# Decay sums of a selective-state scan: one f32 product against three products of exact bfloat16 parts

## The chip, the cores and the metric

The kernel runs on one core of one Trainium2 chip. The metric is the device time of one execution in microseconds. A core has a matrix engine (TensorE, PE in the profile, with its weight loads shown apart as PEld), a vector engine (DVE), a scalar engine (ACT), a general engine (POOL), and SP, which issues the DMA transfers. Each engine runs its instructions in order, and they meet through semaphores. SBUF is the on-chip memory of 128 partitions, PSUM the accumulators that TensorE writes.

## The reference

One layer of a model on 16 sequences of 32 tokens with 512 channels, all in float32, in three stages: a graph attention over a context, a Mamba-2 scan, and a feed-forward part with low-rank additions. The change lies in the scan, cut here to what it concerns:

```python
dt = jax.nn.softplus(dt + dt_bias)                 # per token and head, 128 heads
A = -jnp.exp(A_log)
Ac = (A * dt) ...                                  # one number per token and head
L = jnp.exp(segsum(Ac))                            # L[i, j] = exp(sum of Ac over j < t <= i), 0 for j > i
M = jnp.einsum('bcihn,bcjhn->bcijh', Ch, Bh) * L   # 8 groups of 16 heads share B and C
Y_diag = jnp.einsum('bcijh,bcjhp->bcihp', M, hid * dt)
y = Y_diag + D * hid
y = y * silu(gate), normalized within each group, then the output projection
```

A sequence has 32 tokens, shorter than one chunk, so the part that passes states between chunks contributes nothing.

## The kernel before

The 512 tokens lie as four blocks q of 128 tokens (four sequences each). The 8192 inner channels are 64 tiles t of 128 channels, two heads each; a group g has TG = 8 such tiles. The code is written with a tile framework: the program allocates tiles from pools and calls engine operations, and at compile time a scheduler orders every engine's instructions by the order of the program and by when, in its own model, operands and buffers are ready. It also inserts the semaphores. An engine's order on the chip is then fixed.

Before the groups, `scan_part` loads constants and makes the two masks on POOL: `le`, 1 where token j comes no later than token i in the same sequence, and `gt`, 1 where a token comes later. `lei` is `le` folded to 128 x 32: for each token of a block, which of the 32 positions of its sequence are at or after it. It projects `dt` and makes `dA` = dt times A for all tokens and heads (L1170), and makes `CB` for each group, the product of B and C with the mask (L1186).

Then, for each group, in program order:

- `inner(g + 1)`: for each of the 8 tiles, `project` (L1120) makes the gate and the hidden channels of the next group, each with four f32 matmuls of 128x128 by 128x512, and `convolve` runs the short causal convolution on ACT and DVE (L1127, L1132, L1135). Their PSUM pool has two buffers; the tiles `gs` and `hid` have two buffers of a whole group.
- `mix(g)`: for each tile, four transposes (`pht`, L1228), `hd` on DVE (L1230, dt times the transposed channels), the decays (every second tile, for its four heads), two `el` on DVE (L1241, the decays times `CB`), eight small matmuls `py` (L1249), then `hid` (L1253) and `gs` (L1254) on DVE, their squares on ACT (L1259), and their sum `ssq` on POOL (L1260).
- `close(g)`: `pn` (L1268) sums `ssq` across partitions, DVE and ACT make the inverse norm `gr`, and `po` (L1281) is the output projection, 4 token blocks of 8 f32 matmuls, each accumulated into `xt` by DVE (L1284). Its PSUM pool has two buffers.

`decays(h)` serves four heads, that is a pair of tiles; it runs 32 times. POOL multiplies `lei` and the `dA` of four heads, both broadcast, into `da`, 128 x 512 in f32 with two buffers (L1208). PE multiplies that by the mask `gt` (L1213), which sums dA over the tokens after j up to i. ACT takes the exponential into `ed` (L1218). An f32 `nc.tensor.matmul` appears in the profile as two matmul instructions and two weight loads.

The PSUM pool `ps_m` that `pl` comes from has two buffers, shared with the transposes.

Of the kernel before, what the change touches and what calls it, by code (L numbers as in the profile page):

```python
# [8 lines left out]
F32 = mybir.dt.float32  # L9
F16 = mybir.dt.float16  # L10
BF16 = mybir.dt.bfloat16
I32 = mybir.dt.int32
AF = mybir.ActivationFunctionType
ALU = mybir.AluOpType
# [4 lines left out]
P = 128  # L19
# [21 lines left out]
H_M, G_M, SEQ = 128, 8, 32  # L41
# [11 lines left out]
def kernel(ctx: ExitStack, tc: tile.TileContext, I, out):  # L53
# [68 lines left out]
    with ExitStack() as cx:  # L122
        scan_part(nc, tc, cx, I, id32, ones, xt, U, rstd, lows)
# [931 lines left out]
def scan_part(nc, tc, cx, I, id32, ones, xt, u, rstd, lows):  # L1055


    sc = cx.enter_context(tc.tile_pool(name="sconst", bufs=1))
    wk = cx.enter_context(tc.tile_pool(name="swk", bufs=2))
    sm = cx.enter_context(tc.tile_pool(name="ssm", bufs=3))  # L1060
# [27 lines left out]
    gt = sc.tile([P, P], F32, name="gt")  # L1088
# [10 lines left out]
    lei = sc.tile([P, SEQ], F32, name="lei")  # L1099
# [47 lines left out]
    dA = sc.tile([P, 4, H_M], F32, name="dA")  # L1147
# [44 lines left out]
    def inner(g):  # L1192
# [9 lines left out]
                next(parts, None)  # L1202
        return gs, hid

    def decays(h):

        da = sm.tile([P, 4, 4, SEQ], F32, tag="da", name=f"da{h}", bufs=2)
        nc.gpsimd.tensor_tensor(  # L1208
            da, lei.unsqueeze(1).unsqueeze(1).to_broadcast([P, 4, 4, SEQ]),
            dA[:, :, h:h + 4].rearrange("p q h -> p h q").unsqueeze(3).to_broadcast([P, 4, 4, SEQ]), ALU.mult,  # L1210
        )
        pl = ps_m.tile([P, 4, 4, SEQ], F32, tag="m", name=f"pl{h}")
        nc.tensor.matmul(  # L1213
            pl.rearrange("p h q i -> p (h q i)"), lhsT=gt, rhs=da.rearrange("p h q i -> p (h q i)"),
            start=True, stop=True,
        )
        ed = sm.tile([P, 4, 4, SEQ], F32, tag="ed", name=f"ed{h}", bufs=2)
        nc.scalar.activation(ed, pl, AF.Exp)  # L1218
        return ed

    def mix(g, gs, hid):

        ssq = wk.tile([P, D], F32, tag="ssq", name=f"ssq{g}")
        for i in range(TG):
# [10 lines left out]
            if i % 2 == 0:  # L1235
                decay = decays(2 * t)
# [197 lines left out]
```

## Time and profile before

| | us |
|---|---|
| median of 3 runs | 2409.86 (2409.17 to 2415.53) |
| profiled execution, its own time | 2416.21 |
| its span, first to last instruction | 2414.5 |
| PE busy | 2190.0 (91%) |
| DVE busy | 1699.6 (70%) |
| ACT busy | 1100.1 (46%) |
| POOL busy | 831.6 (34%) |
| pl, L1213, 64 matmul instructions in the scan | 618 ns each (mean, with matmuls overlapping) |
| da, L1208, 32 POOL instructions | 1269 ns each (mean; 1072 to 1624) |

The graph stage runs to about 1365 us, the scan to about 2310, and the feed-forward part to the end. TensorE's granted clock was 0.971 in the mean and 1.00 through most of the scan. In a timeline, a line gives the start in us from the first instruction, the time taken, the engine, the line of the code, the operation, the tiles written and read, and how many instructions are merged in it; idle time before it stands in brackets with what ended it. Matmuls are pipelined and their ends are modelled, so the distance between starts is the better measure of one.

### The profile page before, as it was taken

What the parts mean: (1) busy time and instruction counts of PE and PEld (TensorE: products, weight loads), DVE (VectorE), ACT (ScalarE), POOL (GpSimd) and SP (SyncE); (2) the same over time, 40 slices, a digit from 0 to 9 for tenths busy, and PEclk for the clock granted to TensorE, in tenths of its full rate; (3) what the DMA queues carried; (4) which work ended last, traced back from release to release, by engine and by line L of the source; (5) the groups of instructions that cost most, each with busy time, mean ns of one, the idle gap of its engine ahead of it and who ended that gap; (6) DMA issues with size and microseconds to landing.
All of it is one profiled execution on the core that took longest, in us unless ns stands there. A gap on an engine that the chain in (4) does not pass through costs nothing. (4 is left out here: it accounts for less than half of the span.)

```text
span 2414.5 us, 88867 instructions
## 1 busy us (share of the span) xinstructions
PE 2190.0 (91%) x39234; PEld 1248.1 (52%) x39234; DVE 1699.6 (70%) x3674; ACT 1100.1 (46%) x2023; POOL 831.6 (34%) x897
## 2 busy tenths in 40 slices
PE   5699798999999778789999789999999999999979
PEld 2255455667676454567777544444444444444422
DVE  8487797888899888889999866554553625446643
ACT  6677566667665334345555322333332424333331
POOL 2165556445446565664655300020210202021200
PEclk9799899999999999999999899999999999999989
DMA  1323232132132231422211212213112121210000
GB/s 48 80 55 77 48 80 57 43 73 47 36 70 56 54 77 46 91 52 65 63 34 41 91 53 77 75 32 91 53 53 71 35 91 46 73 55 20 27 36 18
DMA packets 121625, 137.99 MB, mean 57 GB/s; under 512 B 18398, under 2 KB 79506, under 8 KB 121154
## 3 DMA queue, kind: packets, MB, share of 16 engines
q1 hardware_dynamic: 121240, 132.32, 21.9%
q8 instruction: 308, 5.05, 0.9%
q14 instruction: 77, 0.63, 0.1%
HBM read 77.02 MB, written 12.85 MB: 37 GB/s over the span
## 5 line engine op out<-in xcount | busy, mean ns | idle before, releaser
L849 POOL TENSOR_TENSOR EN<-e,rz 128x480 f32<-128x480 f32 x344 | 342.4, 995 | 554.4 <-DVE rz L847 430.1
L874 PE MATMUL u<-WA,DD 128*32 128x128 bf16 (+1 forms) x16512 | 418.6, 250 | 26.4 <-issue 26.4
L874 PEld LDWEIGHTS <-DD 128*32 128x32 f16 x16512 | 338.8, 98 | 72.7 <-issue 68.5
L879 ACT COPY us<-u 128x512 f32<-128x512 f32 x516 | 302.0, 587 | 149.5 <-PE u L874 131.8
L834 ACT ACTIVATE e<-s,smc 128x480 f32<-128x480 f32 x344 | 227.6, 662 | 290.7 <-PE s L829 248.0
L770 POOL TENSOR_TENSOR DD<-fs,crep 128x480 f16<-128x480 f32 (+2 forms) x344 | 349.6, 1017 | 0.0
L902 PEld LDWEIGHTS h<-e,us 128*32 128x32 f32 (+1 forms) x11008 | 248.8, 126 | 144.1 <-issue 65.6
L902 PE MATMUL h<-e,us 128*32 128x30 f32 (+1 forms) x11008 | 282.0, 211 | 37.1 <-DVE e L855 19.4
L821 DVE TENSOR_REDUCE c<-s 128x16 bf16<-128x480 f32 x344 | 220.7, 642 | 107.0 <-PE s L812 104.4
L1132 DVE SCALAR_TENSOR_TENSOR cyh<-ppch,t_conv_w,cyh 128x496 f32<-128x496 f32 (+2 forms) x192 | 137.4, 716 | 221.7 <-ACT cyh L1127 217.7
L1208 POOL TENSOR_TENSOR da<-lei,dA 128x512 f32<-128x512 f32 x32 | 40.6, 1269 | 611.8 <-PE pl L1213 577.5
L1281 PE MATMUL po<-wo,gs 128*128 128x512 f32 x512 | 240.5, 605 | 10.4 <-DVE xt L1284 10.3
L1120 PE MATMUL ppch<-hT,winch 128*128 128x512 f32 x512 | 232.2, 593 | 0.0
L1120 PE MATMUL ppg<-hT,wing 128*128 128x512 f32 x512 | 231.9, 593 | 0.0
L855 DVE STREAM_TRANSPOSE e<-EN 128x512 f32<-128x512 f32 x344 | 224.4, 652 | 0.0
L841 DVE TENSOR_REDUCE z<-e 128x16 f32<-128x480 f32 x344 | 219.5, 638 | 0.0
L539 ACT ACTIVATE sgn<-kd 128x512 bf16<-128x512 f32 x256 | 153.0, 598 | 56.2 <-PE kd L538 52.4
L812 PEld LDWEIGHTS <-DD 128*32 128x32 f16 x5504 | 81.7, 96 | 163.2 <-issue 129.5
L723 DVE TENSOR_SCALAR oh<-it,rank 128x512 bf16<-128x512 f16 x512 | 158.0, 368 | 7.5 <-PE pp L689 7.5
L812 PE MATMUL s<-DX,DD 128*32 128x120 f16 x5504 | 143.1, 223 | 19.6 <-DMA DX<-DD 16.2
L1120 PEld LDWEIGHTS ppch<-hT,winch 128*128 128x128 f32 x512 | 93.7, 190 | 122.7 <-issue 122.3
L1120 PEld LDWEIGHTS ppg<-hT,wing 128*128 128x128 f32 x512 | 95.8, 190 | 114.0 <-issue 114.0
(327 smaller groups left out, 2845.6 us busy)
## 6 DMA issues: line engine op xcount, KB each, us to landing
DX<-DD SPq DMA_DIRECT2D x456, 90.0 KB
wo<-in_out_proj SPq DMA_DIRECT2D x64, 256.0 KB
wing<-in_in_proj SPq DMA_DIRECT2D x64, 256.0 KB
winch<-in_in_proj SPq DMA_DIRECT2D x64, 256.0 KB
crep<-dC SPq DMA_DIRECT2D x128, 64.0 KB
dS<-so SPq DMA_DIRECT2D x32, 256.0 KB
fs<-dS SPq DMA_DIRECT2D x128, 64.0 KB
wincB<-in_in_proj SPq DMA_DIRECT2D x8, 256.0 KB
```

The source lines that it names most:

```text
L770: nc.gpsimd.tensor_tensor(d[:, :, m0 - n0:n1 - n0], win, crep[:, :, m0:n1].unsqueeze(3).to_broadcast([P, 4, n1 - m0, K]), ALU.subtract,)
L812: nc.tensor.matmul(s[rh, j * 4 * QB:(j + 1) * 4 * QB].rearrange("p (b q) -> p b q", b=4), lhsT=d[:, h, c0:c0 + 32], rhs=dx[:, h, :, c0:c0 ...
L821: nc.vector.tensor_reduce(c, live["s", at, gi].rearrange("p (i q) -> p i q", q=QB), AX.X, ALU.max, negate=True)
L834: nc.scalar.activation(e, s.rearrange("p (i q) -> p i q", q=QB), AF.Exp, scale=smc)
L841: nc.vector.tensor_reduce(z, e, AX.X, ALU.add)
L849: nc.gpsimd.tensor_tensor(en[:, :, :QB], e, rz.unsqueeze(2).to_broadcast([P, NI, QB]), ALU.mult)
L855: nc.vector.transpose(e.rearrange("p i q -> p (i q)"), en.rearrange("p i q -> p (i q)"))
L874: nc.tensor.matmul(u[rh, jj], lhsT=d[:, h, c0:c0 + 32], rhs=WA[k][:, h].rearrange("p b o -> p (b o)"), start=(jj == 0 and k == 0), stop=(k ...
L879: nc.scalar.copy(us[:, j - jj:j + 1], u)
L902: nc.tensor.matmul(h[r:r + co, pr, q0:q0 + QB], lhsT=us[:, j, b * co:(b + 1) * co], rhs=e[:, 4 * j + b, :QB], start=npair > 1, stop=True, ...
L1120: nc.tensor.matmul(pp, lhsT=w[:, k], rhs=hT[:, k], start=(k == 0), stop=(k == 3))
L1281: nc.tensor.matmul(po, lhsT=gs[:, i, q * P:(q + 1) * P], rhs=wo[i], start=(i == 0), stop=(i == TG - 1))
```

## The change

`dA` is split once into three bfloat16 tiles that add up to it: the rounded value, the rounded rest, and the rounded rest of that. The masks, zeros and ones, are copied to bfloat16. For each pair of tiles POOL now makes three products `da0`, `da1`, `da2` in bfloat16, each with two buffers of its own (3 x 2 x 1 KB a partition for 2 x 2 KB), and PE runs three bf16 matmuls that accumulate in the same PSUM tile where one f32 matmul ran. `spread(h)`, which makes the products, is called for the first pair at its own `decays`, and for every later pair at the end of the `decays` of the pair before it.

```diff
+    dA3 = []
+    rest = sc.tile([P, 4, H_M], F32, name="dA_rest")
+    nc.vector.tensor_copy(rest, dA)
+    for k in range(3):
+        t = sc.tile([P, 4, H_M], BF16, name=f"dA3_{k}")
+        nc.vector.tensor_copy(t, rest)
+        if k < 2:
+            nc.vector.tensor_tensor(rest, rest, t, ALU.subtract)
+        dA3.append(t)
+    leib = sc.tile([P, SEQ], BF16, name="leib")
+    nc.vector.tensor_copy(leib, lei)
+    gtb = sc.tile([P, P], BF16, name="gtb")
+    nc.vector.tensor_copy(gtb, gt)
+    summands = {}
+
+    def spread(h):
+
+        summands[h] = []
+        for k in range(3):
+            da = sm.tile([P, 4, 4, SEQ], BF16, tag=f"da{k}", name=f"da{h}_{k}", bufs=2)
+            nc.gpsimd.tensor_tensor(
+                da, leib.unsqueeze(1).unsqueeze(1).to_broadcast([P, 4, 4, SEQ]),
+                dA3[k][:, :, h:h + 4].rearrange("p q h -> p h q").unsqueeze(3).to_broadcast([P, 4, 4, SEQ]), ALU.mult,
+            )
+            summands[h].append(da)
+
     def decays(h):
 
-        da = sm.tile([P, 4, 4, SEQ], F32, tag="da", name=f"da{h}", bufs=2)
-        nc.gpsimd.tensor_tensor(
-            da, lei.unsqueeze(1).unsqueeze(1).to_broadcast([P, 4, 4, SEQ]),
-            dA[:, :, h:h + 4].rearrange("p q h -> p h q").unsqueeze(3).to_broadcast([P, 4, 4, SEQ]), ALU.mult,
-        )
+        if h == 0:
+            spread(0)
         pl = ps_m.tile([P, 4, 4, SEQ], F32, tag="m", name=f"pl{h}")
-        nc.tensor.matmul(
-            pl.rearrange("p h q i -> p (h q i)"), lhsT=gt, rhs=da.rearrange("p h q i -> p (h q i)"),
-            start=True, stop=True,
-        )
+        for k, da in enumerate(summands.pop(h)):
+            nc.tensor.matmul(
+                pl.rearrange("p h q i -> p (h q i)"), lhsT=gtb, rhs=da.rearrange("p h q i -> p (h q i)"),
+                start=(k == 0), stop=(k == 2),
+            )
         ed = sm.tile([P, 4, 4, SEQ], F32, tag="ed", name=f"ed{h}", bufs=2)
         nc.scalar.activation(ed, pl, AF.Exp)
+        if h + 4 < H_M:
+            spread(h + 4)
         return ed
```

The split and the two copies stand in the program after `CB` and before the first `inner(0)`.

## The prediction

> **What bounds the kernel now.** I read the page first, then the stretches, then the engine timelines of one burst of the scan.
>
> ```profile
> PE 2190.0 (91%) x39234; PEld 1248.1 (52%) x39234; DVE 1699.6 (70%) x3674; ACT 1100.1 (46%) x2023; POOL 831.6 (34%) x897
> ...
> L1208 POOL TENSOR_TENSOR da<-lei,dA 128x512 f32<-128x512 f32 x32 | 40.6, 1269 | 611.8 <-PE pl L1213 577.5
> ```
>
> The product that the change rewrites is a small POOL group: 32 instructions, and POOL's idle time before them ends when PE has read the buffer two calls back (da has two). So POOL is already ahead of PE, and PE doesn't wait for it. The stretches of the scan:
>
> ```profile
> 1720.00:1820.00 100.00, 98.82 (x353) 46.05 (x353) 49.74 (x70) 32.59 (x48) 13.60 (x10) 1.00 0.21 63
> ...
> 2020.00:2120.00 100.00, 98.76 (x333) 45.41 (x331) 45.46 (x69) 34.12 (x49) 11.98 (x9) 1.00 0.22 64
> ```
>
> PE is busy 98.8 us of 100 while DVE is busy half the time. That average hides two phases. A group takes 105 us (the first pl of a burst starts at 1785.32 and the next such at 1890.4). For some 70 us of it PE runs projections and the output product, with nothing in its way. For some 33 us (the burst, 1785 to 1818 here) `mix` runs, and there DVE has no gap. DVE in that burst, one line an instruction (start, length, idle before in brackets):
>
> ```profile
> 1801.75 0.68 DVE L1241 TENSOR_TENSOR el<-ed,CB 128x512 f32<-128x512 f32 x1
> 1802.35 0.73 DVE L1253 SCALAR_TENSOR_TENSOR hid<-hid,t_Dp,py 128x512 f32<-128x512 f32 x1
> 1803.01 1.10 DVE L1241 TENSOR_TENSOR el<-ed,CB 128x512 f32<-128x512 f32 x1
> 1804.04 0.68 DVE L1254 TENSOR_TENSOR gs<-gs,hid 128x512 f32<-128x512 f32 x1
> 1804.64 0.68 DVE L1230 TENSOR_TENSOR hd<-pht,dt 128x512 f32<-128x512 f32 x1
> 1805.24 0.67 DVE L1241 TENSOR_TENSOR el<-ed,CB 128x512 f32<-128x512 f32 x1
> 1806.02 0.75 DVE L1253 SCALAR_TENSOR_TENSOR hid<-hid,t_Dp,py 128x512 f32<-128x512 f32 x1
> 1806.68 0.92 DVE L1241 TENSOR_TENSOR el<-ed,CB 128x512 f32<-128x512 f32 x1
> 1807.52 1.56 DVE L1254 TENSOR_TENSOR gs<-gs,hid 128x512 f32<-128x512 f32 x1
> 1809.00 0.68 DVE L1230 TENSOR_TENSOR hd<-pht,dt 128x512 f32<-128x512 f32 x1
> ```
>
> and POOL beside it:
>
> ```profile
> 1802.10 1.47 POOL L1260 TENSOR_TENSOR ssq<-ssq,sq 128x512 f32<-128x512 f32 x1 [1.41 <-ACT sq L1259]
> 1805.59 1.46 POOL L1260 TENSOR_TENSOR ssq<-ssq,sq 128x512 f32<-128x512 f32 x1 [2.02 <-ACT sq L1259]
> 1807.12 1.41 POOL L1208 TENSOR_TENSOR da<-lei,dA 128x512 f32<-128x512 f32 x1
> ```
>
> A tile is hd, el, hid, el, gs. By start to start an undisturbed el, gs or hd takes 0.60 us and hid 0.66, so a clean tile is 4 x 0.60 + 0.66 = 3.06 us. The tile from el 1801.75 to el 1805.24 took 3.49: the el that ran against ssq took 1.03 instead of 0.60. The next, to 1809.60, took 4.36: its gs ran against da and took 1.48. So el and gs, whose two inputs both lie in SBUF, wait while POOL works; hd and hid, which read PSUM, keep their 0.68 and 0.74 beside it. An ssq costs DVE 0.43 us a tile and a da 0.87 more. And POOL waits too: a da takes 1.07 us at 1411, where DVE is idle, and 1.41 here. PE in the same stretch:
>
> ```profile
> 1804.89 1.09 PE L1249 MATMUL py<-el,hd 128*64 128x128 f32 x14
> 1805.91 1.12 PE L1213 MATMUL pl<-da,gt 128*128 128x512 f32 x2
> 1806.96 0.43 PE L1249 MATMUL py<-el,hd 128*64 128x128 f32 x2
> ...
> 1808.38 1.09 PE L1249 MATMUL py<-el,hd 128*64 128x128 f32 x14
> ```
>
> py needs el. The el of 1805.24 ended at 1805.91 and its py came at 1806.96; the el of 1806.68 ended at 1807.60 and its py came at 1808.38. Over this burst PE is behind DVE by 0.3 to 1.2 us and no more, and its order is fixed at compile time: a DVE that is later than that stops PE, with the output product behind the waiting py.
>
> **The change, part by part.**
>
> *The product.* A call loses two f32 matmul instructions and gains three bf16 ones. The price is in the chain of the last stage:
>
> ```profile
> 2402.42 0.86 PE fpo L1377 x2
> 2403.28 0.22 PE fpo L1378
> ```
>
> Two f32 instructions of 512 columns 0.86 us, one bf16 0.22. So 0.86 - 3 x 0.22 = 0.20 us a call, 32 calls: 6.4 us less PE work. The nearest row above it: from pl to the next start in the burst was 1.05 (1805.91 to 1806.96), which would make 0.39 a call and 12.5 in all. Three bf16 weight loads of 0.10 replace two of 0.19 beside the matmuls: nothing. Where DVE sets the pace, a shorter pl only lets PE wait earlier. About 8 of the 32 pl stand outside bursts (those at 1517 and 1632, and the first of each later burst); I count 8 x 0.20 = 1.6 us as gained, and keep 12.5 as the end.
>
> *The operands.* 32 POOL instructions become 96. No POOL row reads bf16. The nearest rows say that the type doesn't matter: a memset of 512 elements takes 525 ns in f32 and 522 in bf16, a 480-element multiply 995 ns into f32 and 1032 into f16. I take 1.07 us alone; it could be up to the 1.6 of a disturbed da now. 64 more of them are 68 us on an engine 12 to 14% busy there, so POOL doesn't become the bound. But they go into the bursts. Each da waits for its buffer, which pl frees, so after the change each pl releases three instructions where it released one. Issuing them a pair earlier in the program doesn't move that, since they still wait for the same pl. Of the 64 extra, 4 are made around 1411 to 1420 (DVE waits for PE there), 4 after the pl of 1517 and 1632 (DVE has slack there), some 10 after the first pl of a burst, where DVE is at hd and the convolution, which read PSUM. That leaves 46, or 56 with those ten.
>
> The price of one extra da on DVE: below, 0.43 (what ssq costs a tile); above, 0.87 (what one da costs). Three in a row alternate with el and gs while hd and hid slip past, so I take the middle, 0.65. 46 x 0.65 = 30 us of DVE. PE's lag hides 0.5 of it in each of 8 bursts, 4 us. What remains on the path: 26 us. Low end: 46 x 0.43 - 8 x 1.2 = 10. High end: 56 x 0.87 - 2 = 47.
>
> The Trainium skill's page "SBUF — State Buffer", section "Who interferes with whom", says that GpSimd and VectorE share one pair of ports as an exclusive lock, taken for a whole instruction, by a VectorE instruction with two SBUF inputs among others. The waits of el and gs above agree in kind, but not in full length; if each extra da blocked DVE for its whole 1.07 us, 46 of them would make 49 us, and the time would end some 20 us above my forecast.
>
> *POOL's queue.* ssq stands behind the das. Three das last 3.2 us alone and about 4.5 alternating with DVE; an ssq comes every 3.5 to 4.4 us, so one is late by up to a tile and the next catches up. The last pl of a burst is three tiles before its end, so the final ssq, which pn and then the norm wait for (0.9 us now), is on time. Nothing; if it is not, 2 us a group, 16.
>
> *The splits before.* Six DVE instructions of 128x512 (four copies or casts at 0.46, two subtractions at 0.68) and two small ones at 0.2: 3.6 us. They need dA, made at 1411, and DVE then idles 3.77 us until the product CB. Nothing; 3.6 if that cover is taken by other work.
>
> *Memory.* The new tiles move the addresses of the scan's pools, and so which loads wait for the graph stage to let go. SP's queue has a hole of about 2 us there (1369.4 to 1371.6), so I allow 3 us either way and take 0.
>
> **Sum.** 26 - 1.6 = +24; I shade it to +22, since the compiler plans the order anew for the shorter pl and may put more of the output product where PE would wait. The profiled execution took 2416.2 us (span 2414.5 and 1.7 around it), 6.3 above the median of the three runs. Against it 2438; against the median of 2409.9 it is 2432.
>
> **Rivals.**
>
> *PE keeps what it saves.* POOL's extra work falls where DVE has room, and 6.4 to 12.5 us come off. For it: PE is the busiest engine in every stretch, and DVE is idle half the time. Against: the bursts. It decides if DVE's delay in a burst stays under the lag of 1.2 us plus the 0.8 that four pl save, that is under 2.0 / 5.75 = 0.35 us for an extra da, below even ssq's 0.43. Time: 2397 to 2410.
>
> *POOL is dearer than I think.* A bf16 da of 1.6 us alone holds el and gs longer, and ssq falls behind. 46 x 1.07 = 49, plus 16 for late norms, less 4: some +45 to +60, 2455 to 2470. For it: no row of POOL reads bf16 with a broadcast. Against: the two type comparisons above.
>
> *The change does nothing that shows.* The new order spreads the das into the 70 us between bursts, and gain and loss cancel within 7 us. For it: POOL idles up to 70 us at a stretch there. Against: those idles end at a pl of the next burst, since the two buffers are full. 2403 to 2417.
>
> **How the numbers follow.** Forecast (DVE held up, +10 to +44, so 2420 to 2454): 0.70. PE keeps its saving: 0.12. Dearer POOL: 0.08. Nothing shows: 0.10. No change means within 0.3%, about 7 us, which is what a measurement of this kernel can tell. Faster takes 0.08, three quarters from the first rival and the rest from the last; no change takes 0.14, slower 0.78. The range leaves out about 0.1 on each side: 2406 to 2455.
>
> **What would show it.** Right: 96 POOL da of about 1.07 us undisturbed; el's and gs's means up from 857 and 888 ns towards 1000 and more, with hd and hid unchanged; bursts 3 us longer and groups of 108 us; waits of PE on el above the 34 us of now (29.1 at the weight load, 4.9 at the matmul); pl three instructions 0.22 apart. Wrong: el and gs as they are now, or bursts no longer than before, or a last ssq that pn waits for much over 0.9 us.

## The result

The changed kernel took 2451.06 us in the median of six runs, the kernel before 2417.19 beside it. The ratio is 1.0152 (95% interval 1.0124 to 1.0181), that is 30 to 44 us slower. The same file measured again gave 1.0127 (1.0104 to 1.0151), 25 to 36 us slower. The forecast was slower by 22 us with a time of 2432 in a range of 2406 to 2455: the direction and the mechanism held, the size was too small by about a third. The 2432 was counted from 2409.9; the kernel before took 2417.2 beside the changed one, so 7 of the 19 us between 2432 and 2451 are its own.

The profiled execution took 2445.12 us, its span is 2443.1, against 2414.5 before. From its page:

```profile
PE 2186.7 (90%) x39266; PEld 1248.6 (51%) x39266; DVE 1732.5 (71%) x3682; ACT 1099.3 (45%) x2023; POOL 911.7 (37%) x961
...
L1226 POOL TENSOR_TENSOR da<-leib,dA 128x512 bf16<-128x512 bf16 x96 | 124.3, 1320 | 595.0 <-PE pl L1238 557.1
```

PE has 3 us less to do, POOL 80 us more and DVE 33 us more, although DVE got only eight short instructions. POOL's products still wait for pl, as they did. The two DVE groups with both inputs in SBUF, before and after (busy us, mean ns):

```profile
L1241 DVE TENSOR_TENSOR el<-ed,CB 128x512 f32<-128x512 f32 x128 | 108.1, 857 | 6.1 <-PE py L1249 5.0 <-ACT ed L1218 1.1
...
L1254 DVE TENSOR_TENSOR gs<-gs,hid 128x512 f32<-128x512 f32 x64 | 56.8, 888 | 0.4
```

```profile
L1268 DVE TENSOR_TENSOR el<-ed,CB 128x512 f32<-128x512 f32 x128 | 132.1, 1044 | 4.4 <-PE py L1276 4.4
...
L1281 DVE TENSOR_TENSOR gs<-gs,hid 128x512 f32<-128x512 f32 x64 | 57.9, 905 | 0.3
```

el grew from 857 to 1044 ns, 24 us of DVE time; hid and hd kept 740 and 681 ns. And PE now waits for el. The matmul's own waits from the first burst on, before and after (total us, times, longest):

```profile
PE py L1249 <- DVE el L1241: 4.9, 10, 1.4
```

```profile
PE py L1276 <- DVE el L1268: 25.9, 39, 2.0
```

In the trace nearly all of it lies in the scan. From the first pl to the last accumulation into xt it took 798.1 us before and 825.3 after; a group in the middle takes 108.7 us instead of 105.1. The graph stage, the feed-forward part and the output differ by less than 1 us between these two executions. A burst of the changed kernel, DVE first (start, length, idle before):

```profile
1809.96 1.32 DVE L1268 TENSOR_TENSOR el<-ed,CB 128x512 f32<-128x512 f32 x1
1811.20 1.56 DVE L1281 TENSOR_TENSOR gs<-gs,hid 128x512 f32<-128x512 f32 x1
1812.68 0.68 DVE L1257 TENSOR_TENSOR hd<-pht,dt 128x512 f32<-128x512 f32 x1
1813.28 0.73 DVE L1280 SCALAR_TENSOR_TENSOR hid<-hid,t_Dp,py 128x512 f32<-128x512 f32 x1
1813.94 1.53 DVE L1268 TENSOR_TENSOR el<-ed,CB 128x512 f32<-128x512 f32 x1
```

```profile
1808.17 1.53 POOL L1287 TENSOR_TENSOR ssq<-ssq,sq 128x512 f32<-128x512 f32 x1 [4.86 <-ACT sq L1286]
1809.66 4.03 POOL L1226 TENSOR_TENSOR da<-leib,dA 128x512 bf16<-128x512 bf16 x3
1813.65 1.26 POOL L1287 TENSOR_TENSOR ssq<-ssq,sq 128x512 f32<-128x512 f32 x1
```

```profile
1821.37 1.09 PE L1276 MATMUL py<-el,hd 128*64 128x128 f32 x14
1824.42 0.40 PE L1276 MATMUL py<-el,hd 128*64 128x128 f32 x2 [1.96 <-DVE el L1268]
1824.75 1.98 PE L1308 MATMUL po<-wo,gs 128*128 128x512 f32 x4
```

The three products run from 1809.66 to 1813.69. Within that stretch el and gs, 0.68 us alone, take 1.32 and 1.56, and the three products take 4.03 instead of 3.1 us: the two engines take turns. hd and hid run at full pace beside them. The third line of the last fence shows what it costs: at the next batch of products (1819.70) PE stands still for 1.96 us with the output product behind the waiting py. In the whole scan before, PE had ten such waits, the longest 1.4 us.

### The profile page after: what moved, and what is told of

Read it like the earlier page. It is cut to its first block, busy times and chain, and to the rows that moved or that the text cites. A ratio compares the mean times of both kernels' runs of the same rounds, so it can differ in the third digit from the quotient of the medians.

```text
span 2443.1 us, 88984 instructions
## 1 busy us (share of the span) xinstructions
PE 2186.7 (90%) x39266; PEld 1248.6 (51%) x39266; DVE 1732.5 (71%) x3682; ACT 1099.3 (45%) x2023; POOL 911.7 (37%) x961
## 5 line engine op out<-in xcount | busy, mean ns | idle before, releaser
L1226 POOL TENSOR_TENSOR da<-leib,dA 128x512 bf16<-128x512 bf16 x96 | 124.3, 1320 | 595.0 <-PE pl L1238 557.1
L1120 PEld LDWEIGHTS ppg<-hT,wing 128*128 128x128 f32 x512 | 95.9, 190 | 111.8 <-issue 110.3
```

The lines of the kernel that those rows point to most:

```text
L1120: nc.tensor.matmul(pp, lhsT=w[:, k], rhs=hT[:, k], start=(k == 0), stop=(k == 3))
```

## The experiments

Changes are in us against the kernel before, run beside each kernel on the same chip, with the 95% interval.

### Is it POOL's products, or PE?

The prediction's account, that POOL's extra products hold up el and gs at the SBUF ports and the bursts then wait for DVE, is called the port theory here. Two rivals to it: the three matmuls and weight loads cost PE more than their sum says, or the order that the compiler planned anew is worse. The kernel one_product leaves POOL with one product a call, two_products with two, one_matmul leaves PE with one matmul, and f32_thrice gives the kernel before three products.

one_product:

```diff
-        for k in range(3):
+        for k in range(1):
             da = sm.tile([P, 4, 4, SEQ], BF16, tag=f"da{k}", name=f"da{h}_{k}", bufs=2)
...
-        for k, da in enumerate(summands.pop(h)):
+        for k, da in enumerate(summands.pop(h) * 3):
```

> The changed kernel with one POOL product a call instead of three; the three bf16 matmuls all read it (the two small parts of dA are left out, so the sums are three times the first part). Port theory (POOL's extra products hold up el and gs, and the bursts are bound by DVE): back to the kernel before, -7 to +3 us against it, el and gs means near 860 and 890 ns. PE theory (the three matmuls and weight loads, or the new order of PE, cost the time): still +25 to +37 us.

Measured: +1.0 (-3.4 to +5.1). The whole loss is gone with two of the three products, although PE still runs three bf16 matmuls. el's mean is 882 ns, gs's 795. This kernel is worth more than its time says, because in the middle groups PE runs the same 182 instructions besides pl in the same order from the second pl of a burst to pn. The beginning and end of that stretch, in the changed kernel and in this one:

```profile
1798.56 0.81 PE L1238 MATMUL pl<-da,gtb 128*128 128x512 bf16 x3
...
1834.95 1.05 PE L1295 MATMUL pn<-ones,ssq 128*128 128x1 f32 x8
```

```profile
1796.70 0.81 PE L1238 MATMUL pl<-da,gtb 128*128 128x512 bf16 x3
...
1829.31 1.05 PE L1295 MATMUL pn<-ones,ssq 128*128 128x1 f32 x8 [0.25 <-POOL ssq L1287]
```

36.4 us against 32.6, with PE's work and order equal. So neither PE's work nor its order makes the 3.8 us; POOL's six extra products in that stretch do, at 0.63 us each.

two_products:

```diff
-        for k in range(3):
+        for k in range(2):
             da = sm.tile([P, 4, 4, SEQ], BF16, tag=f"da{k}", name=f"da{h}_{k}", bufs=2)
...
-        for k, da in enumerate(summands.pop(h)):
+        for k, da in enumerate(summands[h] + summands.pop(h)[1:]):
```

> The changed kernel with two POOL products a call; the third matmul reads the second product again (so the smallest part is left out and the second counted twice). Port theory, with a price of about 0.63 us for each extra product in a burst, as the difference between the changed kernel and the one with one product gives: half of their distance, +13 to +17 us against the kernel with one product and so about +13 to +18 against before. If the third product alone does the harm (POOL's queue running late): nearly as fast as before, 0 to +5.

Measured: +20.5 (+14.7 to +26.3), above the expected range, with an interval that reaches into it. The order of PE is again the same, and the stretch takes 35.7 us. So the price isn't even: the second product costs 3.1 us a burst, the third 0.7. DVE loses as unevenly: its el and gs in the stretch take 20.1, 23.8 and 24.1 us with one, two and three products. Why isn't shown.

one_matmul:

```diff
-        for k in range(3):
-            da = sm.tile([P, 4, 4, SEQ], BF16, tag=f"da{k}", name=f"da{h}_{k}", bufs=2)
+        da = sm.tile([P, 4, 4, SEQ], BF16, tag="da0", name=f"da{h}", bufs=2)
+        for k in (2, 1, 0):
             nc.gpsimd.tensor_tensor(
...
-                start=(k == 0), stop=(k == 2),
+                start=True, stop=True,
```

> The changed kernel with its three POOL products, written one after the other into the same tile, and one bf16 matmul (two parts are left out of the sum). Port theory: PE's saving of 2 x 0.22 us a call falls where DVE sets the pace, so +20 to +37 us against before, like the changed kernel. PE theory: 14 us below the changed kernel's best case, that is -14 to 0 us against before.

Measured: +15.2 (+11.6 to +18.9), between the two ranges expected. The products alone make it slower, as the port theory has it. But the two matmuls that are gone, 32 x 2 x 0.22 = 14 us of PE work, came off nearly whole (the changed kernel stood at +30.7 in the same comparison), where I had expected them to be lost in waits. Its middle groups take 106.8 us against 108.7, 1.9 less, and PE has 4 x 0.44 = 1.8 less to do in them. Here PE's order is another one (the third pl of a burst stands before py instead of within it), so this run doesn't say whether PE's time counts in such a burst or whether the order made room for it.

f32_thrice:

```diff
-        nc.gpsimd.tensor_tensor(
-            da, lei.unsqueeze(1).unsqueeze(1).to_broadcast([P, 4, 4, SEQ]),
-            dA[:, :, h:h + 4].rearrange("p q h -> p h q").unsqueeze(3).to_broadcast([P, 4, 4, SEQ]), ALU.mult,
-        )
+        for _ in range(3):
+            nc.gpsimd.tensor_tensor(
+                da, lei.unsqueeze(1).unsqueeze(1).to_broadcast([P, 4, 4, SEQ]),
+                dA[:, :, h:h + 4].rearrange("p q h -> p h q").unsqueeze(3).to_broadcast([P, 4, 4, SEQ]), ALU.mult,
+            )
```

> The kernel before, whose POOL product is made three times into the same f32 tile; PE's work is that of before. Port theory: +28 to +42 us, at least what the change costs, since the f32 matmul stays. PE theory, or a theory that it is the bf16 type of POOL's operands: within 5 us of before.

Measured: +25.6 (+18.9 to +32.2), a middle group 108.6 us. Two further products of the old kind, with PE's work untouched, cost nearly what the change costs. In a middle burst PE also keeps the order of the kernel before, from the second pl to pn, and takes 36.0 us for 32.5. The type of the operands is not the cause. It came out a little below what I had expected.

### Does it matter when POOL works, and what it does?

between: the changed kernel with a group's twelve products held back until the norm of the group before.

```diff
-    def spread(h):
+    def spread(h, mask):
...
-            da = sm.tile([P, 4, 4, SEQ], BF16, tag=f"da{k}", name=f"da{h}_{k}", bufs=2)
+            da = sm.tile([P, 4, 4, SEQ], BF16, tag=f"da{k}", name=f"da{h}_{k}", bufs=4)
             nc.gpsimd.tensor_tensor(
-                da, leib.unsqueeze(1).unsqueeze(1).to_broadcast([P, 4, 4, SEQ]),
+                da, mask.unsqueeze(1).unsqueeze(1).to_broadcast([P, 4, 4, SEQ]),
...
-        if h == 0:
-            spread(0)
...
-        if h + 4 < H_M:
-            spread(h + 4)
...
         rstd(sm, rs, mean, 4, f"gn{g}")
+        if g + 1 < G_M:
+            mask = sm.tile([P, SEQ], BF16, tag="mask", name=f"mask{g}", bufs=2)
+            nc.vector.tensor_scalar(mask, leib, rs[:, 0:1], 0.0, ALU.mult, ALU.is_gt)
+            for h in range(16 * (g + 1), 16 * (g + 2), 4):
+                spread(h, mask)
...
+    for h in range(0, 16, 4):
+        spread(h, leib)
     cur = inner(0)
```

The mask equals `leib`, since the inverse norm is positive; it is there for the wait alone.

> The changed kernel with all its work, but the twelve products of a group are made after the norm gr of the group before, that is in the stretch in which DVE runs convolutions (four buffers a part instead of two; a mask copied by DVE behind gr holds them back). Port theory: the bursts lose the products altogether, also the one a call that the kernel before has there; PE's smaller product counts again: -8 to -30 us against before, el and gs means below 857 and 888 ns. If the cost were the third products themselves on POOL, or the bf16 matmuls, it stays at +25 to +37.

Measured: -3.6 (-8.2 to +1.2). All 96 products and all 96 matmuls are there, and the loss is gone. The twelve products of a group in its trace, and two lines of DVE in the burst before them:

```profile
1832.79 12.36 POOL L1226 TENSOR_TENSOR da<-mask,dA 128x512 bf16<-128x512 bf16 x12 [4.54 <-DVE mask L1298]
```

```profile
1806.46 0.75 DVE L1276 SCALAR_TENSOR_TENSOR hid<-hid,t_Dp,py 128x512 f32<-128x512 f32 x1 [0.73 <-PE py L1272]
...
1809.56 0.75 DVE L1276 SCALAR_TENSOR_TENSOR hid<-hid,t_Dp,py 128x512 f32<-128x512 f32 x1 [0.55 <-PE py L1272]
```

A product takes 1.03 us there from start to start, and in the burst DVE now waits for PE. The stretch from the second pl to pn, still with the same order of PE, takes 31.2 us. With the two runs above, no product in it makes 31.2, one 32.6, two 35.7, three 36.4. The gain stayed below what I had expected. With the bursts free PE is the bound; and in the last group PE waits 2.6 us, once, for a product that was held back. I timed it once more:

> The kernel with the products made between the bursts, timed more closely. Its scan is 7 us shorter than before in the profile, its time 3.6 us with an interval of -8 to +1. Port theory with PE as the bound once the bursts are free: -2 to -8 us.

Measured: -4.1 (-8.2 to +0.2). Two measurements agree on about 4 us, and each interval just includes no change, so a gain over the kernel before is likely but not settled. It is 30 us and more faster than the changed kernel.

f32_between: the kernel before, its f32 products made in the same place.

> The kernel before with its f32 products made in the same place, after gr, in four buffers. Port theory: each call's one product no longer delays el and gs by up to 0.87 us, -5 to -22 us against before. If POOL's products cost nothing in the bursts: within 4 us of before.

Measured: 0.0 (-4.1 to +4.1). My expectation failed, and that teaches the most about the kernel before. The edit did what it should to DVE:

```profile
L1248 DVE TENSOR_TENSOR el<-ed,CB 128x512 f32<-128x512 f32 x128 | 93.7, 744 | 13.3 <-PE py L1256 10.5 <-ACT ed L1225 2.8
...
L1261 DVE TENSOR_TENSOR gs<-gs,hid 128x512 f32<-128x512 f32 x64 | 45.2, 706 | 0.4
```

el and gs together lost 26 us against the kernel before (138.9 for 164.9), and its middle groups take 105.2 us as before. So in the kernel before the one product a call was hidden: PE set the pace. Against the same place in between (103.6 a group) it also gives the price of PE's saving where PE is the bound: 1.6 us a group, 0.40 a call.

memsets: the kernel before, with POOL writing the tile four times ahead of each product.

```diff
+        for _ in range(4):
+            nc.gpsimd.memset(da, 0.0)
         nc.gpsimd.tensor_tensor(
```

> The kernel before with four memsets of the tile da ahead of each product: 2.1 us of POOL's time a call, about as much as the two products that the change adds, but they write and don't read. If el and gs wait for any POOL instruction: +20 to +30 us. If they wait only for one that reads SBUF: within 5 us of before.

Measured: +7.7 (+3.4 to +12.1). A memset took 525 ns, so this is 2.1 us of POOL's time a call. A stretch of its burst, POOL and DVE:

```profile
1795.47 2.27 POOL L1209 MEMSET da<- 128x512 f32 x4 [0.20 <-PE pl L1215]
```

```profile
1795.74 0.68 DVE L1256 TENSOR_TENSOR gs<-gs,hid 128x512 f32<-128x512 f32 x1
1796.34 0.68 DVE L1232 TENSOR_TENSOR hd<-pht,dt 128x512 f32<-128x512 f32 x1
1796.94 0.68 DVE L1243 TENSOR_TENSOR el<-ed,CB 128x512 f32<-128x512 f32 x1
```

gs and el run beside the memsets in 0.68 us, and their means over the run are 859 and 873 ns, those of the kernel before. So el and gs wait for a POOL instruction that reads SBUF and not for one that only writes it. The Trainium skill's page "SBUF — State Buffer", section "SBUF: two separate sides", says this of a VectorE instruction with two SBUF inputs; the run agrees. Where the 7.7 us come from instead wasn't settled. In a middle burst it isn't the order of PE, which is that of the kernel before from the second pl to pn, while the stretch takes 33.4 us for 32.5; later products and ssq behind the memsets are a guess.

### What the first profile didn't show

> The changed kernel unaltered, for a second profile. In the first profile its span is 28.6 us above that of before, while its runs were 1.5% (37 us) slower. If the profile tells the whole, its span here is again about 29 us above the kernel before; if some 8 us come from somewhere that one profiled execution didn't show, the span differs by up to 37 and the difference lies outside the bursts of the scan.

Measured: +30.7 (+25.1 to +36.5), and a span of 2439.8. In both profiled executions the change cost less than in the median of the others, so I took three more profiles.

> The changed kernel unaltered, for a third profile. Its two profiled executions are 29 us above the one of before, its other executions about 36 above those of before. If the profile misses a part by chance, an execution of 2450 us will show it as stretches of half clock in the scan (each 3.41 us long, costing 1.7; one and two of them in the middle of the scan so far, against none in before) or as a longer way from the graph to the first pl; groups of 108.7 us otherwise.

> As again_2, a fourth profile of the changed kernel: bursts and groups as in the others, 108.7 us, and any difference of the span in the clock or outside the bursts.

> The kernel before unaltered, for a second profile: groups of 105.1 us, no half clock between the first burst and the end of the scan, and a span within 8 us of 2414.5.

Measured: spans of 2444.0 and 2447.7 for the changed kernel and 2412.8 for the kernel before. The parts of all six executions (us):

| | before | before_again | changed | again | again_2 | again_3 |
|---|---|---|---|---|---|---|
| last write of hT to first pl | 130.5 | 130.3 | 131.6 | 133.0 | 131.7 | 132.8 |
| first pl to last xt | 798.1 | 798.2 | 825.3 | 827.0 | 825.3 | 831.5 |
| a middle group | 105.1 | 105.1 | 108.7 | 108.7 | 108.7 | 108.7 |

Two things come on top of the groups. The way to the first pl is 1.1 to 2.7 us longer. And in the scan the changed kernel has two or three stretches of half clock (one of them of double length), which the kernel before has not in either profile. One of them in the changed kernel, as stretches (the columns are the length, PE, PEld, DVE, ACT and POOL busy, the granted clock, DMA):

```profile
2038.00:2042.00 4.00, 2.02 (x17) 1.07 (x16) 4.00 (x4) 1.43 (x3) 4.00 (x4) 0.96 0.00 0
2042.00:2046.00 4.00, 4.00 (x12) 1.61 (x13) 2.73 (x5) 1.35 (x2) 1.80 (x2) 0.61 0.00 0
2046.00:2052.00 6.00, 6.00 (x37) 3.01 (x34) 3.39 (x5) 1.53 (x3) 1.53 (x2) 1.00 0.01 3
```

```profile
2041.81 0.66 PE L1276 MATMUL py<-el,hd 128*64 128x128 f32 x2 [1.96 <-DVE el L1268]
2042.40 3.30 PE L1308 MATMUL po<-wo,gs 128*128 128x512 f32 x4
```

At the end of PE's wait of 1.96 us for el the clock is halved for 3.41 us, and four matmuls take 3.30 us instead of 1.98. It costs that group 1.6 us (110.3 instead of 108.7). In again the same happened in two bursts, the first of them here:

```profile
1819.54 0.40 PE L1276 MATMUL py<-el,hd 128*64 128x128 f32 x2 [1.96 <-DVE el L1268]
1819.87 3.67 PE L1308 MATMUL po<-wo,gs 128*128 128x512 f32 x4
```

The same wait stands in every middle burst, but the half clock follows only some of them, other ones in other executions. The traces show which. Within an execution the clock changes only at times that lie a whole number of 3.413 us apart (in again the three stretches begin at 1819.89, 2147.57 and 2270.45 us, 96 and 36 times that). Cut on this grid, the five windows that half clock follows in the middle bursts of the four profiles have PE idle for 1.8 to 2.0 us (1816.48 to 1819.89 in again: 1.97). The other fifteen waits are cut by the edge between two windows (1.32 and 0.67 us in the changed kernel's burst at 1933), and no window of theirs has more than 1.8. So the place of the wait on the grid decides in these bursts, with a boundary near 1.8 us, and the grid lies elsewhere in each execution. The Trainium skill's page "TensorE: Matmul & The Clock Gate", section "Part 1: The HAM clock gate (the "warmup" mystery)", has the clock fall to half after an idle window of about 3.4 us and calls the windows free-running. The half clock, the free-running windows and their length of 3.41 us agree; that it takes a whole idle window doesn't, since here some 1.8 us of idle time in one were enough.

The remaining stretches stand in the last groups, behind other waits: in the changed kernel (2273.78 us) behind one of 1.13 us for ssq. Idle time alone doesn't tell there: that window has 1.1 us of it, and one that ends at 2328.5 in again has 1.9 and isn't followed. The runs between, f32_between and memsets have such stretches in their last groups too, so these aren't the change's alone.

again_3 lost 6.2 us more in the scan than the first profile, 6.1 of it in its last two groups, where 6.83 and 3.41 us at half clock stand for the 3.41 us of the first profile, and PE was idle 2.8 us longer. So what an execution loses there changes from one to the next. So does the stage ahead of the table: the last write of hT starts at 1386.9 and 1385.4 us in the two profiles of the kernel before and at 1381.0 to 1388.2 in those of the changed one, with the earliest in again, which so has the shortest span. Whether those of 2450 to 2460 us have more of it can't be seen, since they weren't profiled; that part of the difference stays open.

## Why the prediction was right or wrong

The direction and the mechanism were right, the size too small: +22 us against +30 to +44. The steps that failed are those that put the clock and the way to the first pl at nothing and took off 2 us for the new order; the deduction for PE's lag was too large as well, but a count that was too high made up for it.

**The bound.** Right that the bursts decide and that el and gs wait for POOL. Not right that a DVE later than PE's lag of 0.3 to 1.2 us stops PE already in the kernel before: f32_between took 26 us off DVE and no time followed, so the burst had more room than I read from one burst's starts, and the one product a call had been hidden whole.

**The product.** Right. I counted 1.6 us as gained, with 12.5 as the end where PE sets the pace. one_product's scan is 1.2 us shorter than that of before, and between against f32_between gives 0.40 us a call where the bursts are free, which is that end (0.39).

**The operands.** The term was 46 x 0.65 = 30 us of DVE. Between one product and three, at an equal order of PE, el and gs take 4.0 us longer in a middle burst, 0.66 for each of its six further products, and 27.8 us longer in all (190.0 for 162.2). The price held, and the count was somewhat high; that the price is even did not hold (3.1 us of the burst for the second product, 0.7 for the third). On the path it is 3.8 us a middle burst, 0.63 a product, and 825.3 - 796.9 = 28.4 us over the scan, some 3 of which are two stretches of half clock: 25 are left. Undisturbed, a bf16 product takes 1.06 us and an f32 one 1.07, so the type made no difference, as taken.

**What I took off it.** The step "PE's lag hides 0.5 of it in each of 8 bursts, 4 us" took off too much: 0.2 were hidden in a middle burst (4.0 of DVE, 3.8 of the burst), and 27.8 - 25 = 3 at most in all. The room in a burst had gone to the first product: in the kernel before, its 3.9 us of DVE a burst were hidden whole, and in the changed kernel it costs the burst 1.4 of the 1.8 us that DVE loses. That the forecast's 26 us for the path stand beside a measured 25 is luck, since the count erred the other way. The 2 us that I shaded off because the order is planned anew had no ground: over the stretch that costs the time, the order of PE was the same with one product and with three.

**POOL's queue.** Right: pn's waits for ssq grew from 9.6 us to 11.2 in all.

**The splits.** "Nothing" was wrong. They found DVE idle, but POOL's first products started as soon as the first part was ready, and the later splits waited for them:

```profile
1412.08 0.43 DVE L1211 CAST dA<-dA_rest 128x512 bf16<-128x512 f32 x1
1412.55 0.69 DVE L1213 TENSOR_TENSOR dA_rest<-dA_rest,dA 128x512 f32<-128x512 f32 x1
1413.27 1.18 DVE L1211 CAST dA<-dA_rest 128x512 bf16<-128x512 f32 x1
1414.49 1.44 DVE L1213 TENSOR_TENSOR dA_rest<-dA_rest,dA 128x512 f32<-128x512 f32 x1
1415.96 1.17 DVE L1211 CAST dA<-dA_rest 128x512 bf16<-128x512 f32 x1
1417.06 0.68 DVE L1186 TENSOR_TENSOR CB<-pcb,le 128x512 f32<-128x512 f32 x1
```

The same cast takes 0.43 us once and 1.18 and 1.17 after that. CB came at 1417.06 instead of 1414.73, of which dA's later end explains 0.6; the way to the first pl grew by 1.1 to 2.7 us. That the splits make all of it wasn't tested.

**Not in the sum:** the half clock, about 3 us in two of the profiles and more in the others. Only the stretches behind PE's new waits for el, 1.6 to 1.7 us each, are the change's for certain; how much of those in the last groups is chance stays open.

Put together from the profiles: 25 for the products without the half clock, less the 1 that the smaller product brings, 1 to 3 on the way to the first pl, and 3 to 9 for the half clock with what follows from it, is 28 to 36. The four profiled spans lie 26 to 34 us above the mean of the two of before; the timed runs gave 31 and 37. The forecast's 22 was 26 - 1.6, less the 2 shaded off, with nothing for the last two terms. The ends of its band weren't worked out alike: the +10 is the operands' term without the 1.6 that the sum takes off, which would make it +8.

**The rivals.** PE keeping its saving is what between shows, and only once POOL's products leave the bursts. A dearer POOL was wrong in its price (the products are as long as before), and ssq was on time.

## What to carry to other kernels

Before work moves onto an idle engine, look for the stretch in which it will run and not at the share of busy time: POOL was busy for 118 of the 798 us of the scan before, 15%, and its further products cost 25 us and more here, since they became ready in the one stretch where DVE had no gap. Held back by a data dependency until that stretch was over, the same products left the kernel no slower than before, with one wait of 2.6 us for them in the trace. Price an added instruction by what its neighbours' durations do when they overlap with it, and don't deduct slack twice: what hid the first instruction hardly hid the second here. A saving on the busiest engine counts only in the stretches which that engine bounds.

## What the runs showed of the hardware

- A POOL instruction that reads SBUF and a DVE instruction with two SBUF inputs take turns: el and gs go from 0.68 us to 1.3 to 1.56 in the burst shown, while memsets of the same tile leave it at 0.68. DVE instructions with one input in PSUM aren't touched (hid 740 ns, hd 681).
- A cast from f32 to bf16 on DVE with one SBUF input also waited for POOL's products (0.43 to 1.18 us).
- A wait of PE of 1.96 us was enough for half clock for the next 3.41 us, in one or two of the five middle bursts that have this wait: those in which a window of the 3.413 us grid held 1.8 to 2.0 us of idle time. Where the grid's edge cut the wait, with at most 1.8 in one window, the clock stayed whole.
